# Layer-0 centring in 64x64 blocks, gated GpSimd passes, and half a ladder step moved to GpSimd in a two-layer convolution-shaped kernel

## The chip, the cores and the metric

The kernel runs on one core of a Trainium2 chip. Its engines work side by side, each through its own instructions in order: TensorE (PE, matmuls into PSUM), VectorE (DVE), ScalarE (ACT), GpSimd (POOL), and SyncE (SP), whose queue here issues nearly all DMAs. The metric is the device time of one execution in microseconds; less is better.

## The reference

x has the shape (16, 32, 128, 128). Layer 0 adds to x an attention over its normalised channels. Layer 1 normalises again, cuts each image into windows of 8x8 pixels with 32 channels, normalises over the channels, and runs three small networks on the windows (rows, columns, channels), the sum of which goes through a fourth. Each small network is a layer norm, eight Gaussian bumps of every value, and a matrix:

```python
def _fastkan(x, ln_g, ln_b, ws, wb, bb):
    ln = _layernorm(x, ln_g, ln_b)
    basis = jnp.exp(-((ln[..., None] - GRID) / DENOM) ** 2)
    flat = basis.reshape(*basis.shape[:-2], -1)
    return flat @ ws.T + jax.nn.silu(x) @ wb.T + bb
...
y = _layernorm(wins, pn_g, pn_b)
a = _fastkan(a, k1...)      # y with window columns turned to rows
d = _fastkan(d, k2...)      # y along window rows
e = _fastkan(y.reshape(b, WS * WS, C), k3...)
z = _fastkan((a + d + e).reshape(b, WS * WS, C), k4...)
out = z + wins
...
x = x + _L0_conv_ref(_gn(x), ...)
x = x + _L1_conv_ref(_gn(x), ...)
```

## The kernel before, in words

First, in the ramp, the kernel reads x once for the sums that layer 0's attention needs, and folds the whole attention and the residual into a 256x256 matrix (`pts`) for each half of the batch. The rest is layer 1 with that matrix in front, in 64 units. A unit is 128 partitions (4 images of 32 channels) by 1024 elements (8 image rows of 128 pixels, that is, one row of 16 windows).

A unit goes through these tasks; the names are those of the functions and of the order lists.

- `load` fetches x for two units. `layer0_norm` multiplies by `pts` (L1068), writes the result `xh` (L1078), subtracts the channel mean with a 128x128 matrix (L1083, two matmuls of 512 columns, each recorded as two), copies that to `xc` (L1092), squares it (L1095), and sums the squares (L1036, with Ln and Exp at L1044 and L1045). `keep` sends `xh` to DRAM, and `again` brings it back when the unit ends.
- `rows_norm` makes y from `xc` on VectorE (L1130). GpSimd adds a bias to it in place (L1134) and then writes a second copy with the window columns turned (L1138). Both lie in one tile, `yy`. `move` regroups `yy` by DMA into `d`; `silus` and `move_silu` do the like for the SiLU.
- Chain a (`norm_a`, `scale_a`, `seed_a`, `ladder_a`, `pair_a`) runs the row and column networks on `d`. Chain b runs the channel network of unit n and the fourth network of unit n - 2 together. `norm` centres by matmuls, evicts twice on ScalarE (L1195), squares (L1198), and spreads the scale with matmuls (L1204); `scale` multiplies on VectorE (L1221).
- The bumps are not computed one by one. `seed` makes the first (in chain a also the fifth) on ScalarE, and a ratio R. `ladder` gets each next bump on VectorE from the one before (L1250), 128x2048 elements each: six steps in chain a, seven in chain b. A step is called here by its chain and bump: a1 makes bump 1 of chain a.
- `products` multiplies each bump by its 32x32 weights (L478). `products_a` and `products_b` put a one-element GpSimd memset, a tick, between the matmuls that open a PSUM bank and the others (L1274); `pair_b` has one more (L1410). `pair_b` also adds chain a's result, moved back by DMA, with the 64x64 matmuls `straight` (L1400) and `turned` (L1421).
- `evict_z` copies the three networks' sum to `z`. `result` adds the fourth network to the residual `xh` on VectorE (L1472), and `store` writes it out.

The work of neighbouring units is interleaved. A planner (`Flow`) runs the tasks with estimated times when the program is built and writes each engine's instructions in the order it finds. For the tasks in `ORDER` it does not choose: the table gives each engine's cyclic order as `task.step.units behind`. The tile pools have fixed numbers of buffers; an instruction that needs a buffer, or another engine's result, waits on semaphores.

The ladder step, and the two GpSimd passes over y, are these lines:

```python
STT(t, by, BIG, at, ALU.min, ALU.mult)                                              # L1250
nc.gpsimd.tensor_scalar(y, y, unit, cr["pn_b"], ALU.mult, ALU.add)                  # L1134
nc.gpsimd.tensor_scalar(turned(yy[:, :, 1, :]), straight(y), unit, zero, ...)       # L1138
```

Of the kernel before, what the change touches and what calls it, by code (L numbers as in the profile page):

```python
# [43 lines left out]
LIFT = {"a": 0.0, "b": 80 * math.log(2.0)}  # L44

# [7 lines left out]
LATE = 2  # L53

# [3 lines left out]
        "products_b.3.4 products_b.4.4 products_b.5.4 layer0_norm.0.1 products_b.6.4 products_b.7.4 norm_b.4.3 "  # L58
        "products_b.8.4 products_b.9.4 norm_b.6.3 products_b.10.4 products_b.11.4 layer0_norm.2.1 products_a.0.3 "
        "products_a.2.3 products_a.3.3 layer0_norm.5.1 products_a.4.3 products_a.5.3 norm_a.0.2 products_a.6.3 "  # L60
        "products_a.7.3 norm_b.0.2 products_a.8.3 products_a.9.3 rows_norm.0.1 norm_a.4.2 products_b.0.3 "
        "norm_a.6.2 products_b.2.3 "
    ),
    "ACT": (
        "norm_b.3.3 silus.0.3 seed_a.0.3 seed_a.1.3 seed_a.2.3 norm_b.5.3 layer0_norm.1.1 seed_a.3.3 seed_a.4.3 "
        "evict_z.0.4 seed_b.0.3 layer0_norm.3.1 layer0_norm.4.1 seed_b.1.3 layer0_norm.6.1 seed_b.2.3 norm_a.1.2 "
        "norm_a.2.2 norm_a.3.2 norm_b.1.2 norm_b.2.2 evict_a.0.3 evict_a.1.3 norm_a.5.2 "
    ),
    "DVE": (
        "ladder_a.2.4 ladder_a.3.4 ladder_a.4.4 ladder_a.5.4 ladder_b.0.4 ladder_b.1.4 rows_norm.1.2 ladder_b.2.4 "  # L70
        "scale_a.0.3 scale_a.1.3 ladder_b.3.4 ladder_b.4.4 ladder_b.5.4 ladder_b.6.4 ladder_a.0.3 scale_b.0.3 "
        "scale_b.1.3 result.0.6 ladder_a.1.3 "
    ),
    "SP": (
        "keep.0.1 move.0.2 store.0.6 again.0.5 load.0.0 move_back.0.3 move_silu.0.2 "
    ),
    "POOL": (
        "products_b.1.3 rows_norm.2.1 rows_norm.3.1 products_a.1.2 "
# [173 lines left out]
def conv_preact_kernel(  # L252
# [79 lines left out]
    eps, unit, ones_n = column(), column(), column()  # L332
    nc.vector.memset(eps, EPS)
    nc.vector.memset(unit, 1.0)
    nc.vector.memset(ones_n, 1.0 / S)
    zero, lift = column(), column()
    nc.vector.memset(zero, 0.0)
    nc.vector.memset(lift, LIFT["b"])
# [29 lines left out]
    c0 = const.tile([P, 4, 32], F32, name="c0")  # L368
    TS(c0, quad.unsqueeze(2).to_broadcast([P, 4, 32]), -1.0 / 32, None, ALU.mult)
    TT(c0, c0, ident.rearrange("p (q c) -> p q c", q=4), ALU.add)  # L370
    c0m = c0.rearrange("p q c -> p (q c)")
# [94 lines left out]
    C_R2, C_XB, C_P, C_B0 = range(4)  # L466
# [34 lines left out]
    def layers():  # L501
        with ExitStack() as es:
# [31 lines left out]
            rows3 = lambda t: t.rearrange("p (h w) -> p h w", h=8)  # L534

# [210 lines left out]
            def attention(bp):  # L746
# [258 lines left out]
                STT(qp, gm, cr["k4_bb"], qp, ALU.add, ALU.mult)  # L1005
# [3 lines left out]
                TT(t, t, qp, ALU.add)  # L1009
                for q in range(KK):  # L1010
                    nc.vector.tensor_copy(l0col(bp, q, C_R2), r2[:, q : q + 1])
                    nc.vector.tensor_copy(l0col(bp, q, C_XB), t[:, q : q + 1])
                    for b in range(4):
                        nc.vector.tensor_copy(
                            l0col(bp, q, C_P)[32 * b : 32 * b + 32], p_[32 * (b ^ 1) : 32 * (b ^ 1) + 32, q : q + 1]
                        )
                ps_, = yield step("PE", 0.6, "Y")
                MM(ps_[:, 0, 0:KK], lhsT=c0m, rhs=qp, start=True, stop=True)
                yield step("DVE", 0.3)
                for q in range(KK):  # L1020
                    TS(l0col(bp, q, C_B0), ps_[:, 0, q : q + 1], -1.0, None, ALU.mult)
                give("Y")
# [6 lines left out]
            def rsqrt_rows(src, e, kind):  # L1029

                parts = e.shape[1]
                lr, ve = yield step("PE", 0.24 * parts, kind, "Y")
                for j in range(parts):
                    for c in range(4):
                        u = parts * c + j
                        MM(  # L1036
                            ve[32 * c : 32 * c + 32, 0, 0:P],
                            lhsT=e[:, j, :],
                            rhs=src[:, u * P : (u + 1) * P],
                            start=j == 0,  # L1040
                            stop=j == parts - 1,
                        )
                yield step("ACT", 0.62)
                ACT(lr, ve[:, 0, 0:P], AF.Ln, bias=eps)  # L1044
                ACT(lr, lr, AF.Exp, scale=-0.5)  # L1045
                give("Y")
                return lr
# [13 lines left out]
            def layer0_norm(n):  # L1061
# [19 lines left out]
                xc, yp = yield step("PE", 1.94, "xc", "Y")  # L1081
                for u in range(2):
                    MM(  # L1083
                        yp[:, u, :].rearrange("p (h w n) -> p h n w", h=4, w=8),
                        lhsT=c0m,
                        rhs=xh[:, u * 512 : (u + 1) * 512].rearrange("p (h n w) -> p h n w", h=4, w=8),
                        start=True,
                        stop=True,
                    )
                used(("xh", n), "xh", 2)  # L1090
                yield step("ACT", 1.01, lag=0.0)
                ACT(xc, flat(yp), AF.Identity, bias=l0col(bp, kk, C_B0))  # L1092
                give("Y", LAG)
                sq, = yield step("ACT", 0.96, "n")
                ACT(sq, xc, AF.Square)  # L1095
                lr = yield from rsqrt_rows(sq, e0, "lr0")
                give("n")
                put(("lr0", n), (xc, lr))
# [12 lines left out]
            def rows_norm(n):  # L1111

                yield "get", "parameters"
                xc, lr = yield "get", ("lr0", n)
# [18 lines left out]
                yield step("POOL", 1.29)  # L1133
                nc.gpsimd.tensor_scalar(y, y, unit, cr["pn_b"], ALU.mult, ALU.add)  # L1134
                turned = lambda t: t.rearrange("p w (h n) -> p h w n", h=8)
                straight = lambda t: t.rearrange("p h (w n) -> p h w n", w=8)
                yield step("POOL", 1.29)
                nc.gpsimd.tensor_scalar(turned(yy[:, :, 1, :]), straight(y), unit, zero, ALU.mult, ALU.add)  # L1138
# [86 lines left out]
            def seed(name, n, par):  # L1225
# [3 lines left out]
                for k, i in enumerate(SEEDS[name]):  # L1229
# [8 lines left out]
                    yield step("ACT", 1.9 if LIFT[name] else 1.81, lag=0.0)  # L1238
                    ACT(u, u, AF.Exp, scale=-1.0, **({"bias": lift} if LIFT[name] else {}))  # L1239
                    put(("u", name, n, i), u, LAG)  # L1240

            def ladder(name, n):

                by = yield "get", ("up", name, n)
                for i in range(NG):
                    if i in SEEDS[name]:
                        at = yield "get", ("u", name, n, i)
                        continue
                    t, = yield step("DVE", 2.21, "u", lag=0.0)
                    STT(t, by, BIG, at, ALU.min, ALU.mult)  # L1250
                    used((name, n, i - 1), "u", 2)
                    put(("u", name, n, i), t, LAG)
                    at = t
                give("R", LAG)

# [5 lines left out]
            def products(name, n, wt, also, bank, ws, silus, then, cross):  # L1261
# [14 lines left out]
                for i in range(NG):  # L1276
                    t = yield "get", ("u", name, n, i)
                    yield step("PE", 1.11, lag=0.0)
# [10 lines left out]
                    used((name, n, i), "u", 1 if i + 1 == NG or i + 1 in SEEDS[name] else 2)  # L1289
# [47 lines left out]
            def evict_z(n):  # L1337
                acc = yield "get", ("z_acc", n)
                z, = yield step("ACT", 1.01, "z")
                ACT(z, flat(acc), AF.Identity, bias=cr["k3_bb"])  # L1340
# [14 lines left out]
            def norm_b(n):  # L1355
# [5 lines left out]
                rows = lambda t, h: t[:, 4 * h : 4 * h + 4, 0, :]  # L1361
                cols = lambda t, h: t[:, 512 * h : 512 * h + 512]
                two = (y, rows) if n < N else (z, cols), (z, cols) if n >= BACK else (y, rows)
# [18 lines left out]
            def pair_b(n):  # L1382
# [8 lines left out]
                def straight(acc):  # L1391
# [3 lines left out]
                    for i in range(4):  # L1395
                        v, h = i // 2, i % 2
                        for f in range(2):
# [3 lines left out]
                                    bank(acc, 64 * (f ^ h), 64, 0, h).rearrange("p (l w) -> p l w", l=4)[  # L1401
                                        :, :, 64 * v : 64 * v + 64
                                    ],
                                    lhsT=(near if v else ident)[o, o],
                                    rhs=ar[o, 4 * h : 4 * h + 4, 0, 64 * v : 64 * v + 64],
# [7 lines left out]
                def turned(acc):  # L1413
# [3 lines left out]
                    for h in range(2):  # L1417
                        for f in range(2):
# [3 lines left out]
                                    bank(acc, 64 * (1 ^ f ^ h), 64, 0, h).rearrange("p (h w n) -> p w h n", h=4, w=8),  # L1422
                                    lhsT=(near if h else ident)[o, o],
                                    rhs=ar[o, :, 1, 64 * h : 64 * h + 64].rearrange("p w (h n) -> p w h n", h=4),
# [13 lines left out]
                def silus(o, q):  # L1438
# [5 lines left out]
                    v = mine[o, 4 * h : 4 * h + 4, 0, :] if mine is t else rows3(mine)[o, 4 * h : 4 * h + 4, :]  # L1444
                    return v.rearrange("p h (w n) -> p h w n", w=8) if k else v
# [21 lines left out]
            def result(n):  # L1467
# [3 lines left out]
                yield step("DVE", 1.2)  # L1471
                STT(xh, xh, l0col(bp, kk, C_P), flat(acc), ALU.mult, ALU.add)  # L1472
# [3 lines left out]
            def store(n):  # L1476
                bp, kk, j = units[n]
                xh = yield "get", ("result", n)
                yield step("SP", 2.6, lag=0.0)
                for b in range(4):  # L1480
                    nc.sync.dma_start(
                        out=out_rows[bp * KK + kk, b, :, :, j * RB : (j + 1) * RB],
                        in_=xh[32 * (b ^ 1) : 32 * (b ^ 1) + 32, :],
                    )
                late = fl.moved(1.4, 2.0)
                give("xh", late)

            def again(n):
# [3 lines left out]
                for b in range(4):  # L1492
                    nc.sync.dma_start(out=xh[32 * b : 32 * b + 32, :], in_=xd[32 * (b ^ 1) : 32 * (b ^ 1) + 32, :])
# [5 lines left out]
            with tc.manual_schedule(engines=IN_ORDER):  # L1499
# [23 lines left out]
                        every("keep", keep),  # L1523
                        every("layer0_norm", layer0_norm),
# [88 lines left out]
```

## Time and profile before

| | |
|---|---|
| median of 3 runs | 2687.7 us (2686.57 to 2696.28) |
| profiled execution: its own time | 2688.95 us |
| its span (first to last instruction) | 2687.2 us |
| granted TensorE clock, mean | 0.987 |
| VectorE ladder steps (L1250), 846 in all | 2292 ns each |
| VectorE `scale` (L1221), four a unit | 1214 ns each |
| GpSimd pass L1134 / L1138, median | 2768 / 1200 ns |
| ScalarE Exp on 128x2048 with a bias column / without (L1239) | 1989 / 1904 ns |

A row of the timeline gives the start in us, the duration in us, the engine, the line, the operation, output<-inputs with sizes, and how many instructions of the kind the row merges; in brackets, how long the engine was idle before it and what ended that. A row of the waits gives who waited for whom, then us in total, the number of times and the longest. The pitch of an instruction is the time from its start to the next one's start on the same engine: it can be shorter than its duration, since neighbours overlap by some 0.08 us.

### The profile page before, as it was taken

How to read it: one execution, taken by the hardware profiler on the slowest of the kernel's cores; microseconds unless marked ns; L12 is line 12 of the kernel's file. 1: busy time of each engine (PE TensorE's matmuls, PEld its weight loads, DVE VectorE, ACT ScalarE, POOL GpSimd, SP SyncE). 2: the span in 40 equal slices, each digit the busy share in tenths (PEclk: the TensorE clock that was granted, in tenths of full speed). 3: DMA queues.
4: the chain of work that ended last, by engine and by line, in shares of the span. 5: the costliest groups of instructions: out<-in, count | busy, mean ns of one | idle time of the engine just before them, and what ended most of it. 6: DMA issues, size and time to landing. Idle time of an engine off the chain costs nothing.

```text
span 2687.2 us, 123945 instructions
## 1 busy us (share of the span) xinstructions
PE 2553.4 (95%) x56611; PEld 1300.7 (48%) x56611; DVE 2492.0 (93%) x1637; ACT 2340.5 (87%) x1967; POOL 320.6 (12%) x431
## 2 busy tenths in 40 slices
PE   6998999999999999999999999999999999999975
PEld 6884444444444444444444444444444444444432
DVE  5755799999999999999999999999999999999987
ACT  0016699999999999999999999999999999999973
POOL 4300000111101111101111011111011111011100
PEclk9998999999999999999999999999999999999988
DMA  9752345555555555555555555545555555555421
GB/s 252 189 140 64 104 119 146 144 146 148 146 142 152 151 144 140 144 144 145 147 142 150 143 151 147 146 136 149 141 152 145 142 150 142 150 150 148 135 85 45
DMA packets 289706, 379.71 MB, mean 141 GB/s; under 512 B 42400, under 2 KB 239520, under 8 KB 289184
## 3 DMA queue, kind: packets, MB, share of 16 engines
q1 hardware_dynamic: 275968, 352.48, 47.5%
q10 hardware_dynamic: 9504, 16.85, 2.4%
q8 instruction: 446, 7.31, 1.2%
q0 software_dynamic: 3712, 2.46, 0.4%
q14 instruction: 76, 0.62, 0.1%
HBM read 103.18 MB, written 67.11 MB: 63 GB/s over the span
## 4 chain that ended last, share of the span: by engine, by line
PE 80%; DVE 7%; issue 5%; DMA 1%; ACT 1%; POOL 0%; DVEq 0%; ACTq 0%; POOLq 0%
PE X L478 41%; PE Y L1068 9%; PE Y L1204 5%; PE Y L1083 5%; PE Y L478 4%; PE Y L1036 4%; PE X L498 3%; DVE u L1250 3%; DVE yy L1130 3%; PE Y L1119 2%; PE X L1400 2%; PE X L1421 2%; PE X L733 1%; DMA xh<-xh 1%; DVE yc L1221 0%
## 5 line engine op out<-in xcount | busy, mean ns | idle before, releaser
L1250 DVE SCALAR_TENSOR_TENSOR u<-R,u 128x2048 f32<-128x2048 f32 x846 | 1923.8, 2292 | 54.2 <-PE X L478 5.9
L478 PE MATMUL X<-u,wt_a 32*32 32x512 f32 x16384 | 690.4, 600 | 31.7 <-POOL vec L1274 26.4
L478 PE MATMUL X<-u,wt_b 32*32 32x512 f32 x16896 | 608.1, 601 | 13.0 <-DVE u L1250 12.2
L478 PEld LDWEIGHTS X<-u,wt_a 32*32 32x32 f32 x16384 | 297.5, 103 | 279.1 <-issue 94.9
L1231 ACT ACTIVATE u<-yc,vec 128x2048 f32<-128x2048 f32 x194 | 387.4, 1997 | 24.8 <-DVE yc L1221 17.8
L478 PEld LDWEIGHTS X<-u,wt_b 32*32 32x32 f32 x16896 | 228.0, 103 | 289.1 <-issue 123.1
L1221 DVE TENSOR_TENSOR yc<-yc,Y 128x1024 f32<-128x1024 f32 x260 | 304.9, 1214 | 9.1 <-PE Y L1204 9.0
L1195 ACT ACTIVATE yc<-Y 128x1024 f32<-128x1024 f32 x260 | 251.0, 1018 | 24.1 <-PE Y L478 24.0
L1234 ACT ACTIVATE R<-yc,vec 128x2048 f32<-128x2048 f32 x130 | 258.5, 1988 | 0.0
L1198 ACT ACTIVATE u<-yc 128x2048 f32<-128x2048 f32 x130 | 247.5, 1904 | 2.1
L1239 ACT ACTIVATE u<-u 128x2048 f32<-128x2048 f32 x128 | 243.7, 1904 | 2.0
L1068 PE MATMUL Y<-x,pt 128*128 128x512 f32 x512 | 240.1, 612 | 2.2 <-DVE yy L1130 1.3
L1274 POOL MEMSET vec<- 128x1 f32 x130 | 12.9, 99 | 1524.4 <-PE X L498 1509.7
L1134 POOL TENSOR_SCALAR yy<-yy,vec,col_r 128x1024 f32<-128x1024 f32 x64 | 168.6, 2634 | 157.0 <-DVE yy L1130 132.4
L733 PE MATMUL X<-R 128*64 128x257 f32 (+3 forms) x2048 | 151.5, 308 | 24.0 <-DVE R L707 22.4
L1068 PEld LDWEIGHTS Y<-x,pt 128*128 128x128 f32 x512 | 93.2, 192 | 147.0 <-issue 143.0
L733 PEld LDWEIGHTS X<-R 128*64 128x64 f32 x2048 | 140.7, 140 | 38.0 <-DVE R L707 25.1
L1317 ACT ACTIVATE ad<-X,col 128x1024 f32<-128x1024 f32 x128 | 135.7, 1120 | 0.3 <-PE X L478 0.2
L1239 ACT ACTIVATE u<-u,vec 128x2048 f32<-128x2048 f32 x66 | 131.3, 1989 | 0.0
L478 PE MATMUL Y<-yy,c 32*32 32x512 f32 x1056 | 129.2, 598 | 1.2 <-DVE att L894 1.2
L1083 PE MATMUL Y<-xh,c 128*128 128x512 f32 x256 | 129.3, 628 | 1.0 <-DVE yc L1221 0.7
L1152 ACT ACTIVATE S<-yy 128x2048 f32<-128x2048 f32 x64 | 122.5, 1913 | 0.7
(224 smaller groups left out, 2825.7 us busy)
## 6 DMA issues: line engine op xcount, KB each, us to landing
xh<-xh SPq DMA_DIRECT2D x512, 128.0 KB
d<-yy SPq DMA_DIRECT2D x512, 128.0 KB
sd<-S SPq DMA_DIRECT2D x512, 128.0 KB
ad_r<-ad SPq DMA_DIRECT2D x512, 128.0 KB
x<-in_x SPq DMA_DIRECT2D x256, 128.0 KB
out<-xh SPq DMA_DIRECT2D x256, 128.0 KB
u<-in_x ACTq DMA_DIRECT2D x28, 256.0 KB
u<-in_x SPq DMA_DIRECT2D x28, 256.0 KB
```

Of the source, the lines that this page charges most:

```text
L478: MM(dst(to, g_), lhsT=wt[32 * g_ : 32 * g_ + 32, :], rhs=rhs(g_, to ^ cross[g_]), start=start, stop=stop,)
L733: MM(g[64 * q : 64 * q + 64, k, lo:hi], lhsT=t[:, b, at : at + 64], rhs=t[:, b, lo:hi], start=first, stop=last,)
L1068: MM(xp[:, u, :], lhsT=pts[bp][:, k, kk * P : (kk + 1) * P], rhs=xr[:, k, u * 512 : (u + 1) * 512], start=k == 0, stop=k == KK - 1,)
L1083: MM(yp[:, u, :].rearrange("p (h w n) -> p h n w", h=4, w=8), lhsT=c0m, rhs=xh[:, u * 512 : (u + 1) * 512].rearrange("p (h n w) -> p h n w ...
L1134: nc.gpsimd.tensor_scalar(y, y, unit, cr["pn_b"], ALU.mult, ALU.add)
L1195: ACT(v[:, i * RB : (i + 1) * RB], flat(yt[i]), AF.Identity)
L1198: ACT(sq, v, AF.Square)
L1221: TT(v[:, o], v[:, o], flat(rb[i]), ALU.mult)
L1231: ACT(u, v, AF.Square, bias=bqs[k])
L1234: ACT(up, v, AF.Exp, bias=bp_, scale=2.0)
L1239: ACT(u, u, AF.Exp, scale=-1.0, **({"bias": lift} if LIFT[name] else {}))
L1250: STT(t, by, BIG, at, ALU.min, ALU.mult)
```

## The change

1. Layer-0 centring. The 128x128 matrix `c0m` gives way to 64x64 blocks (`c0w`, one for each half of the batch and channel group), so that four tiles of TensorE work on 512 columns each. The block carries a scale of 1/(1 + sd), and `xh` is scaled so that `result` needs no multiplication. The two halves of the columns come out with partition halves exchanged in one of them; `straight`, `turned`, `norm_b`'s operands, `silus`' operands, `evict_z`, `again`, `result` and `store` follow that layout. `turned` issues 8 matmuls of 256 columns for 4 of 512, `result` 2 instructions of 512 for one of 1024, `store` 8 DMAs for 4 of twice the size.
2. ScalarE squares from PSUM, before a new task `centre` copies to `xc`; the two were the other way round.
3. GpSimd's passes over y. The turned copy comes first and includes the bias; from the third unit on it waits for ladder step b3 of two units earlier (in chain order it is the step just before `scale_a`). The in-place pass follows later.
4. Ladder step a2 is split. VectorE does the second 1024 of the 2048 columns; a new GpSimd task `assist` does the first 1024 in two instructions, a min and a product, after step a1.
5. Bias columns that hold a constant become immediates (Ln, and chain b's seed Exp).
6. `ORDER` is new. GpSimd's cycle is: turned copy, min, in-place pass, product, two ticks.

```diff
+HALVES = {"a": (2,), "b": ()}
+EARLY = 3
+GATE = ("b", 3)
     "DVE": (
-        "ladder_a.2.4 ladder_a.3.4 ... scale_b.1.3 result.0.6 ladder_a.1.3 "
+        "ladder_b.0.6 ladder_b.1.6 rows_norm.1.4 ladder_b.2.6 scale_a.0.5 scale_a.1.5 ladder_b.3.6 ladder_b.4.6 "
+        "ladder_b.5.6 ladder_b.6.6 ladder_a.0.5 scale_b.0.5 scale_b.1.5 result.0.8 ladder_a.1.5 ladder_a.2.5 "
+        "ladder_a.3.5 ladder_a.4.5 ladder_a.5.5 "
     "SP": (
-        "keep.0.1 move.0.2 store.0.6 again.0.5 load.0.0 move_back.0.3 move_silu.0.2 "
+        "store.0.7 keep.0.2 again.0.6 move_back.0.4 move_silu.0.3 load.0.0 move.0.2 "
     "POOL": (
-        "products_b.1.3 rows_norm.2.1 rows_norm.3.1 products_a.1.2 "
+        "rows_norm.2.3 assist.0.4 rows_norm.3.3 assist.1.4 products_a.1.4 products_b.1.4 "
...
-                ACT(lr, ve[:, 0, 0:P], AF.Ln, bias=eps)
+                ACT(lr, ve[:, 0, 0:P], AF.Ln, bias=EPS)
...
                 for u in range(2):
-                    MM(
-                        yp[:, u, :].rearrange("p (h w n) -> p h n w", h=4, w=8),
-                        lhsT=c0m,
-                        rhs=xh[:, u * 512 : (u + 1) * 512].rearrange("p (h n w) -> p h n w", h=4, w=8),
+                    for f in range(2):
+                        o = slice(64 * f, 64 * f + 64)
+                        MM(
+                            yp[64 * (f ^ u) : 64 * (f ^ u) + 64, u, :].rearrange("p (h w m) -> p h m w", h=8, w=8),
+                            lhsT=c0w[o, bp, kk, :],
+                            rhs=xh[o].rearrange("p (h u m w) -> p u h m w", h=8, u=2, m=8)[:, u],
...
-                ACT(xc, flat(yp), AF.Identity, bias=l0col(bp, kk, C_B0))
-                ACT(sq, xc, AF.Square)
+                ACT(windows(sq), chunks(yp), AF.Square)
+            def centre(n):
+                xc, = yield step("ACT", 1.01, "xc")
+                nc.scalar.copy(windows(xc), chunks(yp))
...
-                nc.gpsimd.tensor_scalar(y, y, unit, cr["pn_b"], ALU.mult, ALU.add)
-                nc.gpsimd.tensor_scalar(turned(yy[:, :, 1, :]), straight(y), unit, zero, ALU.mult, ALU.add)
+                add = nc.gpsimd.tensor_scalar(turned(yy[:, :, 1, :]), straight(y), unit, cr["pn_b"], ALU.mult, ALU.add)
+                if n >= EARLY:
+                    after([add], [before])
+                nc.gpsimd.tensor_scalar(y, y, unit, cr["pn_b"], ALU.mult, ALU.add)
...
+                    if i in HALVES[name]:
+                        t = yield "get", ("open", name, n, i)
+                        yield step("DVE", 1.15, lag=0.0)
+                        STT(t[:, RB:], by[:, RB:], BIG, at[:, RB:], ALU.min, ALU.mult)
+            def assist(n):
+                rc, = yield step("POOL", 1.2, "att", lag=0.0)
+                after([nc.gpsimd.tensor_scalar(rc, by[:, 0:RB], BIG, None, ALU.min)], [before])
+                t, = yield step("POOL", 2.35, "u")
+                nc.gpsimd.tensor_tensor(t[:, 0:RB], rc, at[:, 0:RB], ALU.mult)
...
-                STT(xh, xh, l0col(bp, kk, C_P), flat(acc), ALU.mult, ALU.add)
+                for h, c in enumerate((C_B, C_BX)):
+                    o = slice(512 * h, 512 * h + 512)
+                    STT(xh[:, o], xh[:, o], l0col(bp, kk, c), acc[:, h, :], ALU.add, ALU.add)
```

## The prediction

> **What bounds the kernel now.** I read the page first, then a table by stretches, the waits of the steady part, then the two engines the change trades between, instruction by instruction.
>
> ```profile
> span 2687.2 us, 123945 instructions
> PE 2553.4 (95%) x56611; PEld 1300.7 (48%) x56611; DVE 2492.0 (93%) x1637; ACT 2340.5 (87%) x1967; POOL 320.6 (12%) x431
> ```
>
> The shares include ramp and tail; a steady stretch (columns PE, PEld, DVE, ACT, POOL busy, clock, DMA share, GB/s) says more:
>
> ```profile
> 1500.00:1900.00 400.00, 390.61 (x9048) 187.86 (x9032) 392.35 (x208) 390.29 (x325) 46.65 (x55) 1.00 0.53 147
> ```
>
> Three engines are 97 to 98% busy at full clock. So who waits for whom (us in total, times, longest; 700 to 2300 us, 43.5 units):
>
> ```profile
> PEld X L478 <- DVE u L1250: 75.9, 132, 0.8
> ACT lr L1044 <- PE Y L1036: 27.5, 45, 1.2
> PE X L478 <- POOL vec L1274: 18.4, 43, 0.5
> PE Y L1204 <- DVE yy L1130: 17.4, 43, 0.8
> DVE yc L1221 <- PE Y L1204: 1.2, 4, 0.4
> ```
>
> The others wait for VectorE; VectorE waits for nobody. Its order over one unit:
>
> ```profile
> 1505.43 1.21 DVE L1130 TENSOR_TENSOR yy<-xc,Y 128x1024 f32<-128x1024 f32 x1
> 1506.56 2.29 DVE L1250 SCALAR_TENSOR_TENSOR u<-R,u 128x2048 f32<-128x2048 f32 x1
> 1508.77 2.35 DVE L1221 TENSOR_TENSOR yc<-yc,Y 128x1024 f32<-128x1024 f32 x2
> 1511.03 11.72 DVE L1250 SCALAR_TENSOR_TENSOR u<-R,u 128x2048 f32<-128x2048 f32 x5
> 1522.66 2.35 DVE L1221 TENSOR_TENSOR yc<-yc,Y 128x1024 f32<-128x1024 f32 x2
> 1524.92 1.27 DVE L1472 SCALAR_TENSOR_TENSOR xh<-xh,l0c,X 128x1024 f32<-128x1024 f32 x1
> 1526.12 16.20 DVE L1250 SCALAR_TENSOR_TENSOR u<-R,u 128x2048 f32<-128x2048 f32 x7
> 1542.24 1.21 DVE L1130 TENSOR_TENSOR yy<-xc,Y 128x1024 f32<-128x1024 f32 x1
> ```
>
> Back to back: 1542.24 - 1505.43 = 36.81 us a unit, all of it VectorE. TensorE's need is 36.8 less its two waits (18.4 + 17.4)/43 = 0.8: 36.0. ScalarE's is 36.8 - 27.5/43 = 36.2. About 60 units run at this pace (from 365 us to 2540).
>
> GpSimd has room, but look at how it runs beside VectorE:
>
> ```profile
> 1507.15 2.77 POOL L1134 TENSOR_SCALAR yy<-yy,vec,col_r 128x1024 f32<-128x1024 f32 x1 [0.39 <-DMA xh<-xh]
> 1510.02 1.20 POOL L1138 TENSOR_SCALAR yy<-yy,vec 128x1024 f32<-128x1024 f32 x1
> ```
>
> Same size, 2.77 against 1.20. The first begins inside the ladder step of 1506.56 and makes no progress until that step is over (1508.85): 1.07 us later it is done. The second runs at full speed beside L1221, which reads one operand from PSUM. And the other way round, once, in the ramp:
>
> ```profile
> 233.79 2.59 DVE L1250 SCALAR_TENSOR_TENSOR u<-R,u 128x2048 f32<-128x2048 f32 x1 [0.84 <-ACT u L1239]
> 233.05 1.20 POOL L1134 TENSOR_SCALAR yy<-yy,vec,col_r 128x1024 f32<-128x1024 f32 x1 [47.33 <-DVE yy L1130]
> ```
>
> Here GpSimd came first, kept its 1.20 us, and the ladder step took 2.59 instead of 2.29: held up 0.30, to 234.09, that is 0.15 before GpSimd's recorded end. In the steady part the 0.04 by which the step of 1511.03 is stretched (2.33) is the same, with L1138 ending at 1511.22. So whichever of the two starts first excludes the other. The Trainium skill says so too (SBUF — State Buffer, SBUF: two separate sides).
>
> **The change part by part**, per unit.
>
> *VectorE.* Half a ladder step leaves. Two halves of size 1024 differ by 2.29 - 1.21 (L1250 against L1221), so 1.07 less. `result` becomes two of 512: L1472 goes from a pitch of 1.20 to 2 x 0.67 (0.53 of streaming and its 0.13 fixed), 0.13 more. The half step is followed by step 3, which waits for it and for GpSimd; the ladder's dependent pitch with two waits is 2.39 where this pair's was 2.32: 0.07 more. The 0.04 of L1138 goes, since GpSimd's first pass is now gated to the end of step b3 and fits beside the two `scale_a` (1.20 in 2.26). Sum -0.83; summing the new order pitch by pitch I get 35.91, so -0.89, which I use.
>
> *The wait that comes.* GpSimd's order becomes: turned copy (gated), tick, min (gated to the end of ladder step a1), the y pass, the product, two ticks. The y pass now stands between min and product. Time from the start of a1: VectorE's a1 takes a pitch of 2.20, two `scale_b` 2.26, two `result` 1.33, so the half step could start at 5.80 and step 3 at 7.12. GpSimd: a1 ends at 2.29; with 0.10 between its instructions (1509.92 to 1510.02) min is 2.39 to 3.59, the y pass 3.69 to 4.89, both beside VectorE work with a PSUM operand. The product starts at 4.99, before the half step, and reads two SBUF tensors, so the half step waits for it.
>
> How long is that product? The trace has no tensor_tensor on GpSimd. The nearest row is L1138: 1.20 for 1024 elements, but with one streamed input. By the row the product ends at 6.19, the half step waits 6.19 - 0.15 - 5.80 = 0.24, and the unit changes by -0.65: 39 us faster in all. The Trainium skill (GPSIMD Engine Reference, Performance versus the Vector engine) speaks against this: two inputs share one read port, about 2.6 cycles an element at 1.2 GHz, 4497 ns for 2048. For 1024 my estimate from that is 2.25 (half) to 2.54 (2.22 and L1138's fixed 0.32). I take 2.4, because the second input is a second stream that L1138 lacks. Then the product ends at 7.39, the half step waits 7.24 - 5.80 = 1.44, and the unit changes by -0.89 + 1.44 = +0.55. With 2.25 it is +0.40, with 2.54 +0.69. Break-even is a product of 1.85.
>
> *TensorE.* Centring: L1083 takes 1.98 for its four records (1524.53 to 1526.51 on the chain); four 64x64 tiles over 512 columns are what L1421 issues now, 1.08 (1522.42 to 1523.5). -0.90. `turned` becomes eight half-width matmuls like L1400's (1.09): nothing. New operand strides in runs of 8: no row; 0 to 0.2 each, taken 0. TensorE's need falls to 35.1; it is not the bound, so worth 0 here.
>
> *ScalarE.* A bias column costs 0.085 (L1239: 1989 with, 1904 without). Gone from three Ln, one Exp and the xc copy; the Square reads PSUM (1018 like L1195, was 1059): about -0.47, to 35.7. Also hidden behind VectorE, worth 0; uncovered it would be a bound 0.2 below VectorE's 35.9, so no gain of more than 1.1 a unit is possible in any case. Writing in runs of 8: taken 0.
>
> *Queues.* SP's `store` goes from 4 DMAs (3.01) to 8 half-size ones (6.0). A unit with a load fills SP for 32.6 now, 35.6 then, still under the period. `move` waits for the y pass, which ends at 4.89 instead of long before: on the clock above 1525.4 instead of 1523.0, behind the load in SP. It issues for 5.65, to 1531.0; `norm_a` took the data at 1532.6. That leaves 1.6 for landing; if late, up to 1 us of TensorE's 2 us and ScalarE's 1.6 of slack at the longer period covers it. GpSimd's tick for products_a now stands behind the product (7.49, or 1527.95, against 1527.87): 0.1, covered likewise. `centre` holds a PSUM buffer 1 us longer, but Ln already ended that stretch at 1532. The set-up loses a matmul and gains four small VectorE passes: under 2 us, taken 0.
>
> **Sum.** 60 x 0.55 = +33 us on the profiled execution's 2688.95 (span 2687.2 and 1.75 around it); the median of the runs shown is 1.25 lower, so 2687.7 + 33 = 2721. About 0.5% (13 us) is what a measurement of this kernel can tell from no change.
>
> **The rivals.**
> *The product does not hold up the half step* (it is as cheap as L1138, or two-input operations interleave). For: only one instance of GpSimd coming first by a margin is in the trace, none with this operation. Against: that instance, and all the 2.77s. By the cheap product 39 us faster, 2649; with a product of 2.4 beside the half step, step 3 waits until 7.49 instead of 7.12, the unit changes by -0.89 + 0.37 = -0.52, 31 us faster: 2657. Chance 0.20.
> *Both gains and waits cancel*: a product of 1.7 to 2.0, -0.15 to +0.15 a unit, 2679 to 2697. Chance 0.09.
> *The half step wins the race.* If GpSimd's start, min or y pass takes 0.81 longer in all, the half step runs first and the product stands still until about 6.95, ends at 9.35, and step 3 starts at 9.4 instead of 7.12: -0.89 + 2.3 = +1.4, 2772. For: spans on GpSimd are rough. Against: L1138's 1.20 with a spread of 0.01. Chance 0.08.
> *It is as reckoned*: 0.63, with 2.25 to 2.54 for the product and 0.1 for what I took as 0: 2708 to 2735.
>
> **How the numbers follow.** Faster 0.20, same 0.09, slower 0.63 + 0.08 = 0.71. Range 2655 to 2740: it leaves out the race (0.08) and about half of the faster case.
>
> **What would show it.** Right: the half step's instruction (1024 elements) lasts about 2.6 instead of 1.2, its end 0.1 after the product's; the product about 2.4; period 37.3; TensorE and ScalarE with more waits for VectorE. L1134's successor at 1.2, not 2.77. Wrong: a half step of 1.2; or VectorE with waits for TensorE or ScalarE, which would put the bound elsewhere; or a step 3 that starts long after the half step.

## The result and the profile after

The changed kernel takes 2837.1 us (median of 4 runs, 2833.7 to 2841.0) against 2692.0 for the one before (4 runs): a ratio of 1.0544, with a 95% interval of 1.0516 to 1.0573. It is slower, as forecast, but by 145 us where 33 were forecast, and outside the range (its upper end was 2740). The page of the changed kernel, and its steady stretch (PE, PEld, DVE, ACT, POOL busy, clock, DMA share, GB/s):

```profile
span 2839.1 us, 126157 instructions
PE 2549.1 (90%) x57375; PEld 1322.0 (47%) x57375; DVE 2454.8 (86%) x1696; ACT 2307.0 (81%) x1967; POOL 610.4 (22%) x559
```

```profile
1500.00:1900.00 400.00, 369.19 (x8736) 181.90 (x8736) 365.81 (x206) 363.97 (x310) 87.54 (x72) 0.99 0.54 137
```

No engine is full any more: three that were 97 to 98% busy are at 91 to 92%. GpSimd's two new lines in the page's groups (count, busy us, mean ns, idle before):

```profile
L1291 POOL TENSOR_SCALAR att<-R 128x1024 f32<-128x1024 f32 x64 | 178.1, 2783 | 163.0 <-DVE u L1271 136.7
L1293 POOL TENSOR_TENSOR u<-att,u 128x1024 f32<-128x1024 f32 x64 | 207.6, 3243 | 0.2
```

The min (L1291) takes 2.77 us where 1.20 was reckoned, in all but one of 64 cases within 2.76 to 2.79; the next pass starts 2.87 after it in the rows below, so the length is not only that of a recorded span. The product (L1293) is 2.34 to 2.38 when nothing is in its way, as reckoned. The half step is L1268 here, the other ladder steps are L1271, `scale` is L1235, `result` L1528, the turned copy L1148 and the y pass, the in-place one, L1152. One unit's VectorE and GpSimd around them, from the timeline (start, duration):

```profile
1558.07 2.35 DVE L1235 TENSOR_TENSOR yc<-yc,Y 128x1024 f32<-128x1024 f32 x2
1560.33 1.40 DVE L1528 SCALAR_TENSOR_TENSOR xh<-xh,l0c,X 128x512 f32<-128x512 f32 x2
1561.64 1.72 DVE L1268 SCALAR_TENSOR_TENSOR u<-R,u 128x1024 f32<-128x1024 f32 x1
1565.62 6.89 DVE L1271 SCALAR_TENSOR_TENSOR u<-R,u 128x2048 f32<-128x2048 f32 x3 [2.25 <-POOL vec L1317]
```

```profile
1558.23 2.77 POOL L1291 TENSOR_SCALAR att<-R 128x1024 f32<-128x1024 f32 x1 [2.41 <-DVE u L1271]
1561.10 1.20 POOL L1152 TENSOR_SCALAR yy<-yy,vec,col_r 128x1024 f32<-128x1024 f32 x1
1562.26 3.32 POOL L1293 TENSOR_TENSOR u<-att,u 128x1024 f32<-128x1024 f32 x1
```

The min runs into the time of `result`, so the y pass (L1152) is still on when the half step (L1268, 1561.64) comes: that waits 0.5 for it (1.72 instead of 1.22). By then the product has begun too, and stands still until the half step is through (3.32 instead of 2.38). Step a3 starts at 1565.62, 3.97 after the half step, where 1.32 is its own. In about half of the units `scale_b` comes some 0.6 later, the half step then starts with the product, and it is 3.47. In three of 64 the product wins, which makes the half step 3.2 to 3.5 long.

The waits between 800 and 2400 us (41 units), engines and SP's queue, point to a second loss:

```profile
ACT yc L1209 <- PE Y L481: 118.7, 41, 4.8
PE Y L481 <- DMA d<-yy: 19.7, 14, 2.3
DVE u L1271 <- POOL vec L1317: 85.5, 38, 2.3
DVE yc L1235 <- PE Y L1218: 14.7, 36, 0.8
SPq L1192 <- POOL yy L1152: 96.9, 27, 6.5
```

SP waits 96.9/41 = 2.4 us a unit for the y pass before it can issue `move` (L1192); TensorE then waits for d, and ScalarE stands 118.7/41 = 2.9 us a unit for `norm_a`'s result. An engine with slack may stand without loss; what costs is that VectorE, too, waits for the spread scale of the two `scale` steps, 14.7/41 = 0.4 us a unit. Its wait for L1317, GpSimd's tick that follows the product, 85.5/41 = 2.1, is the product's.

The 152 us between the two profiled spans lie as follows, by the starts of `rows_norm` on VectorE (units counted from 0):

| stretch | before | after | more |
|---|---|---|---|
| to unit 6 | 436.3 | 448.2 | 12 |
| unit 6 to 63 | 2100.9 (36.86 each) | 2219.9 (38.95 each) | 119 |
| from unit 63 to the end | 149.9 | 171.0 | 21 |

### The profile page after: what moved, and what is told of

The parts are those of the page before. It is cut to its first block, busy times and chain, and to the rows that moved or that the text cites. A ratio compares the mean times of both kernels' runs of the same rounds, so it can differ in the third digit from the quotient of the medians.

```text
span 2839.1 us, 126157 instructions
## 1 busy us (share of the span) xinstructions
PE 2549.1 (90%) x57375; PEld 1322.0 (47%) x57375; DVE 2454.8 (86%) x1696; ACT 2307.0 (81%) x1967; POOL 610.4 (22%) x559
## 4 chain that ended last, share of the span: by engine, by line
PE 30%; DVE 28%; POOL 13%; issue 9%; SPq 6%; ACT 5%; DMA 4%; DVEq 0%; ACTq 0%; POOLq 0%
DVE u L1271 24%; PE X L481 15%; POOL u L1293 5%; POOL att L1291 5%; PE Y L481 3%; DVE yc L1235 3%; SPq L1192 2%; POOL yy L1152 2%; PE Y L1036 2%; PE Y L1218 2%; PE Y L1068 2%; DMA out<-xh 2%; PE X L501 2%; DMA d<-yy 2%; PE X L738 1%
## 5 line engine op out<-in xcount | busy, mean ns | idle before, releaser
L1271 DVE SCALAR_TENSOR_TENSOR u<-R,u 128x2048 f32<-128x2048 f32 x782 | 1774.5, 2289 | 194.8 <-POOL vec L1317 132.9
L481 PE MATMUL X<-u,wt_a 32*32 32x512 f32 x16384 | 681.7, 622 | 122.0 <-POOL vec L1317 105.7
L481 PEld LDWEIGHTS X<-u,wt_a 32*32 32x32 f32 x16384 | 323.8, 105 | 360.6 <-issue 145.1
L1253 ACT ACTIVATE u<-u 128x2048 f32<-128x2048 f32 x194 | 368.9, 1902 | 2.0
L1235 DVE TENSOR_TENSOR yc<-yc,Y 128x1024 f32<-128x1024 f32 x260 | 305.3, 1215 | 41.1 <-PE Y L1218 40.4
L1317 POOL MEMSET vec<- 128x1 f32 x130 | 12.6, 97 | 1093.5 <-PE X L501 1093.5
L1291 POOL TENSOR_SCALAR att<-R 128x1024 f32<-128x1024 f32 x64 | 178.1, 2783 | 163.0 <-DVE u L1271 136.7
L1293 POOL TENSOR_TENSOR u<-att,u 128x1024 f32<-128x1024 f32 x64 | 207.6, 3243 | 0.2
L1457 POOL MEMSET vec<- 128x1 f32 x64 | 6.3, 99 | 678.9 <-PE X L1445 678.9
L481 PE MATMUL Y<-d,c 32*32 32x512 f32 x2048 | 83.8, 634 | 53.9 <-issue 24.7
L1148 POOL TENSOR_SCALAR yy<-yy,vec,col_r 128x1024 f32<-128x1024 f32 x64 | 79.8, 1246 | 205.2 <-DVE yy L1140 122.9
```

What stands on the lines that cost most here:

```text
L481: MM(dst(to, g_), lhsT=wt[32 * g_ : 32 * g_ + 32, :], rhs=rhs(g_, to ^ cross[g_]), start=start, stop=stop,)
L1235: TT(v[:, o], v[:, o], flat(rb[i]), ALU.mult)
L1253: ACT(u, u, AF.Exp, scale=-1.0, bias=LIFT[name])
L1271: laid = STT(t, by, BIG, at, ALU.min, ALU.mult)
L1291: after([nc.gpsimd.tensor_scalar(rc, by[:, 0:RB], BIG, None, ALU.min)], [before])
L1293: nc.gpsimd.tensor_tensor(t[:, 0:RB], rc, at[:, 0:RB], ALU.mult)
```

## The experiments

In the table, "a unit" is the mean distance of `rows_norm` on VectorE in the steady part; "a2 to a3" is the mean distance from the start of step a2 (half or whole) to the next step, 20 to 46 units; the own time of a half step there is 1.32, of a whole one 2.32. Each ratio is to the kernel before as it ran beside that kernel (medians 2688.8 to 2692.6). In the code, "..." stands for lines left out.

| kernel | us | ratio to before (95%) | a unit | a2 to a3 |
|---|---|---|---|---|
| before | | 1 | 36.86 | 2.32 |
| changed | 2837.1 | 1.0544 (1.0516 to 1.0573) | 38.96 | 3.67 |
| e1 whole step | 2704.9 | 1.0052 (1.0036 to 1.0069) | 37.25 | 2.32 |
| e2 y pass first | 2767.1 | 1.0279 (1.0263 to 1.0294) | 37.89 | 3.01 |
| e3 cheap pass for min | 2777.2 | 1.0318 (1.0286 to 1.0350) | 37.80 | 2.19 |
| e4 min with columns | 2875.8 | 1.0702 (1.0684 to 1.0720) | 39.57 | 4.38 |
| e5 no min, y pass first | 2682.3 | 0.9971 (0.9958 to 0.9985) | 36.60 | 1.33 |
| e6 whole step, late y pass | 2727.2 | 1.0136 (1.0110 to 1.0162) | 37.45 | 2.32 |
| e7 e5, move_back first | 2690.6 | 0.9997 (0.9988 to 1.0005) | 36.84 | 1.33 |
| e8 e7 without gate | 2685.0 | 0.9987 (0.9978 to 0.9996) | 36.74 | 1.33 |
| e10 e8, move before load | 2639.9 | 0.9811 (0.9797 to 0.9825) | 35.99 | 1.33 |
| e12 e10, again late | 2933.1 | 1.0909 (1.0888 to 1.0929) | 41.08 | 1.33 |
| e13 changed, queue of e10 | 2840.5 | 1.0553 (1.0533 to 1.0572) | 38.83 | 3.72 |
| e14 whole step, queue of e10, no gate | 2688.5 | 0.9985 (0.9976 to 0.9994) | 36.97 | 2.32 |

**The split undone (e1).**

```diff
-HALVES = {"a": (2,), "b": ()}
+HALVES = {"a": (), "b": ()}
-        "rows_norm.2.3 assist.0.4 rows_norm.3.3 assist.1.4 products_a.1.4 products_b.1.4 "
+        "rows_norm.2.3 rows_norm.3.3 products_a.1.4 products_b.1.4 "
...
-                        every("assist", assist),
```

> The change without the split: step a2 is whole on VectorE again, the min and the product on GpSimd are gone, and the y pass follows the gated turned copy at once. Theory A (the min takes 2.77 instead of 1.2, so min, y pass and product hold up the half step and step a3 by 2.2 to 2.6 us a unit): the wait is gone; VectorE has its 36.8 of before, 0.13 more for the two result halves, and up to 0.28 where the y pass reaches into step b4: about 37.1 a unit, 2695 to 2715 us. Rival B (the new column layout, the exchanged order of y passes or the new order of the engines costs the time, the split little): stays above 2780 us, with waits of TensorE and ScalarE as in the changed kernel.

2704.9: 132 of the 145 us are gone, so the loss comes with the split and the order on GpSimd that it brings. The rest, 0.39 a unit against before, is VectorE's own: step b4, which the y pass reaches into, has 0.30 more (2.73 from its start to the next, before 2.43), and the two halves of `result` 0.13.

**The y pass ahead of the min (e2).**

```diff
-        "rows_norm.2.3 assist.0.4 rows_norm.3.3 assist.1.4 products_a.1.4 products_b.1.4 "
+        "rows_norm.2.3 rows_norm.3.3 assist.0.4 assist.1.4 products_a.1.4 products_b.1.4 "
```

> The changed kernel, but GpSimd does the in-place y pass right behind the turned copy, before the min. Theory A: min from 2.39 to 5.16 after the start of step a1, product 5.26 to 7.64, ahead of the half step, which waits until 7.49 instead of 5.80: 1.7 a unit, and 0.28 where the y pass reaches into step b4; about 37.9 a unit against the measured 38.96, 2765 to 2785 us. Rival C (the late y pass, which makes the move to d, norm_a and scale_a late, is the main cost): nearly all comes back, 2690 to 2715 us.

2767.1 and 37.89 a unit, as theory A reckoned (37.9). One unit of it:

```profile
1561.05 2.90 DVE L1268 SCALAR_TENSOR_TENSOR u<-R,u 128x1024 f32<-128x1024 f32 x1
1557.64 2.76 POOL L1291 TENSOR_SCALAR att<-R 128x1024 f32<-128x1024 f32 x1 [2.57 <-DVE u L1271]
1560.49 2.37 POOL L1293 TENSOR_TENSOR u<-att,u 128x1024 f32<-128x1024 f32 x1
```

The product comes first, and the half step lasts 2.90. Step a3 comes 3.01 after the half step's start, 1.69 more than its own 1.32: the time from 5.80 to the product's end. With the min at 2.77 the steady period adds up: 35.91, 0.28 at step b4 and 1.69 make 37.88. VectorE's waits for TensorE, 22.2 us in the changed kernel between 800 and 2400 us, are 0.5 us here.

**A cheap pass in the place of the min (e3), and the min in the cheap pass's form (e4).** A column here is an operand with one value per partition.

```diff
-after([nc.gpsimd.tensor_scalar(rc, by[:, 0:RB], BIG, None, ALU.min)], [before])
+after([nc.gpsimd.tensor_scalar(rc, by[:, 0:RB], unit, zero, ALU.mult, ALU.add)], [before])   # e3
+after([nc.gpsimd.tensor_scalar(rc, by[:, 0:RB], unit, big, ALU.mult, ALU.min)], [before])    # e4
...                                         # e4: a column `big` that holds BIG
```

> The changed kernel with the min replaced by a multiplication by 1 and addition of 0 in the form of the y pass (the bound on R is left out in that half). Theory A (the min itself is slow): the pass takes 1.20, the product starts at 4.99, the half step waits 1.44 as the prediction reckoned: 37.35 a unit plus up to 0.4 of the late y pass, 2720 to 2750 us. Rival D (whatever GpSimd does at that place takes 2.77, because of what VectorE does beside it): the pass takes 2.77 again, 2825 to 2845 us.

> The changed kernel with its min kept, but written like the cheap pass: multiplication by 1 and then min, both operands from columns, so that only the second operation differs from the cheap pass. If the min operation itself is slow on GpSimd: 2.7 or more for 1024 elements, and 2825 to 2850 us as the changed kernel. If the one-operation form with an immediate was slow: 1.20, and 2765 to 2790 us as the cheap pass, with the bound kept.

GpSimd's groups, first of e3, then of e4, where the min is at L1293 (800 to 2400 us):

```profile
L1291 POOL TENSOR_SCALAR att<-R,vec 128x1024 f32<-128x1024 f32 x43 | 51.4, 1196 | 80.6 <-DVE u L1271 80.6
L1293 POOL TENSOR_TENSOR u<-att,u 128x1024 f32<-128x1024 f32 x43 | 101.8, 2368 | 0.0
```

```profile
L1293 POOL TENSOR_SCALAR att<-R,vec 128x1024 f32<-128x1024 f32 x40 | 151.1, 3777 | 68.4 <-DVE u L1273 68.4
```

At the same place, with the same tiles and the same kind of operands, multiply-add takes 1196 ns and multiply-min 3777; the change's min alone takes 2767. So it is the min, not the place and not the form. e4's time, 2875.8, is 26 us above what was expected of a slow min, since this form of it is slower still.

e3 (2777.2) shows the rest too: with the pass at 1.20 and the product at 2.37, the half step is held up 0.87 (2.19 against 1.32). That is less than the 1.44 of the prediction for two reasons. GpSimd's three instructions start 1.17 apart and not 1.30, so the product begins 4.72 after step a1's start, 0.27 sooner than reckoned; and `scale_b` now comes 0.3 late, which GpSimd does not wait for. The unit lands at 37.80, 0.4 above the prediction's 37.4, with further waits ahead of step b1, of `rows_norm` and of both scales. The time is 27 us above the upper end of what theory A expected: in the profiled execution, the fastest of the four at 2767.8, ramp and tail together are 26 us longer than before, and theory A has no place for them.

**The y pass late, by itself (e6).**

```diff
 # on the whole-step kernel e1
+                    late = yield "get", ("late", n - 1)         # step a1
...
-                nc.gpsimd.tensor_scalar(y, y, unit, cr["pn_b"], ALU.mult, ALU.add)
+                pass2 = nc.gpsimd.tensor_scalar(y, y, unit, cr["pn_b"], ALU.mult, ALU.add)
+                    after([pass2], [late])
```

> As the whole-step kernel, but the in-place y pass waits for the end of ladder step a1, as late as in the changed kernel; GpSimd has nothing else there and runs beside scale_b, so no lock on VectorE. What is late alone is the y pass, with the move to d behind it. Theory C1 (the prediction's: covered by slack): VectorE's own 36.94, since step b4 no longer loses 0.33; 2688 to 2706 us, not slower than the whole-step kernel's 2704.9. Theory C2 (not covered: the move, norm_a and the two scale steps run late, as the 1.0 us of other waits a unit in the cheap-pass kernel suggest): 37.5 to 37.9 a unit, 2720 to 2750 us.

2727.2: slower than e1 by 22 us although step b4 gets its 0.33 back, so the late y pass costs 0.5 a unit in the steady part (37.45 against the 36.94 that VectorE needs), and the tail is 14 us longer. That is C2, at its low end. The waits show the way it takes, and SP's queue where it begins (800 to 2400 us):

```profile
ACT yc L1213 <- PE Y L481: 41.8, 28, 4.0
PE Y L481 <- DMA d<-yy: 10.3, 5, 3.0
SPq L1196 <- POOL yy L1154: 41.3, 19, 3.3
```

**Neither min nor late y pass (e5).**

```diff
-                after([nc.gpsimd.tensor_scalar(rc, by[:, 0:RB], BIG, None, ALU.min)], [before])
-                nc.gpsimd.tensor_tensor(t[:, 0:RB], rc, at[:, 0:RB], ALU.mult)
+                after([nc.gpsimd.tensor_tensor(t[:, 0:RB], by[:, 0:RB], at[:, 0:RB], ALU.mult)], [before])
...
-        "rows_norm.2.3 assist.0.4 rows_norm.3.3 assist.1.4 products_a.1.4 products_b.1.4 "
+        "rows_norm.2.3 rows_norm.3.3 assist.0.4 products_a.1.4 products_b.1.4 "
```

> The changed kernel without the min (the product reads R directly, so the bound on R is left out in that half) and with the y pass right behind the turned copy. Theory A: the product runs from 2.39 to 4.77, beside work that has a PSUM operand, the half step is free at 5.80; VectorE 35.91 plus 0.28 for the y pass, 36.2 a unit against 36.86 before: 2645 to 2665 us, faster than before. Rival E (ScalarE or TensorE with the new layout becomes the bound, or the ramp and tail of the changed order, 33 us longer, stay): 2685 to 2720 us.

The lock is gone (1.33 from a2 to a3), and yet it takes 2682.3, 17 us over the upper end of what theory A gave: 36.60 a unit, though 22 of 57 units take theory A's 36.2. Something else holds the others.

**What else: SP's queue (e7, e8, e10, e12).** All four build on e5; the last three also leave the gate out. SP's waits of e5 pointed at the `store`, whose landing `again` (L1550) waits for:

```profile
SPq L1550 <- DMA out<-xh: 210.9, 87, 4.5
```

```diff
-        "store.0.7 keep.0.2 again.0.6 move_back.0.4 move_silu.0.3 load.0.0 move.0.2 "
+        "store.0.7 keep.0.2 move_back.0.4 again.0.6 move_silu.0.3 load.0.0 move.0.2 "   # e7, e8
+        "store.0.7 keep.0.2 move_back.0.4 again.0.6 move_silu.0.3 move.0.2 load.0.0 "   # e10
+        "store.0.7 keep.0.2 move_back.0.4 move_silu.0.3 move.0.2 again.0.6 load.0.0 "   # e12
-EARLY = 3
+EARLY = 10**9                                                                           # e8, e10, e12: no gate
```

> The kernel without min and with the y pass first, and on SP's queue move_back ahead of again. Theory F (again waits 4.9 us a unit for the landing of the store's eight DMAs, move_back stands behind it, so straight and then scale_b are late: 2.40 instead of 2.20 there): scale_b comes on time, 36.58 a unit falls to 36.2 to 36.4, 2658 to 2674 us. Rival G (TensorE or ScalarE is simply full at 36.6): no change, 2677 to 2689 us.

Theory F falls: `scale_b` is as late as before (2.42 after the start of a1, where 2.20 is on time), and the median is not better but 8 us worse. (The execution that was profiled took 2704.0, 13 above the median, so the table's 36.84 is somewhat high.) The largest wait in a queue was not the one that counted.

> The same without the gate on the turned copy, which then starts inside step b3, stands still until its end, and finishes 1.07 after it, as L1134 did before. If the gate costs its hand-over (step b4 waits 0.2 for the y pass): about 0.15 a unit less than with the gate, 8 to 12 us less. If the gate was needed (the pass would start ahead of step b3 or sooner and hold VectorE up): 0.3 to 1 a unit more, 15 us or more above it.

Step b4 comes back to 2.41 from 2.60, as reckoned; part of that is lost again to the other waits: 2685.0, 6 us less where 8 to 12 were expected. Here, where the y pass follows at once, the gate is not needed. Units now lie between 35.93, which is VectorE's own time, and 39. SP's queue of e8 in a unit with a load, and e10's, where `move` (L1192) was put ahead of the `load` (L1058):

```profile
1557.41 4.62 SPq L1058 DMA_DIRECT2D x<-in_x  x8
1562.14 5.66 SPq L1192 DMA_DIRECT2D d<-yy  x8
```

```profile
1527.69 6.04 SPq L1192 DMA_DIRECT2D d<-yy  x8
1533.84 4.84 SPq L1058 DMA_DIRECT2D x<-in_x  x8
```

> The no-gate kernel with move ahead of load on SP's queue. Theory H (in units with a load, move stands behind its eight DMAs, d lands late, and norm_a, ScalarE and the scale steps follow; units of 38 to 39 us come from this): those units go, 36.74 a unit falls to 36.3 to 36.5, 2660 to 2675 us. Rival E (the ring of TensorE's stretch from rb_a to evict_z and ScalarE's from evict_z to the next rb_a, about 36.5 us as the trace adds up, is the bound): little, 2675 to 2687 us, and units of 36.78 stay the commonest.

2639.9, 20 us below what theory H gave, and rival E is refuted: the ring of TensorE and ScalarE that I had added up to 36.5 closes in 35.99. 51 of 57 units take 35.93 to 36.0. The swap issues `move` sooner and `load` later; the two were not tried apart. VectorE's timeline of one of them, and GpSimd's:

```profile
1512.81 1.21 DVE L1140 TENSOR_TENSOR yy<-xc,Y 128x1024 f32<-128x1024 f32 x1
1513.94 2.28 DVE L1271 SCALAR_TENSOR_TENSOR u<-R,u 128x2048 f32<-128x2048 f32 x1
1516.14 2.34 DVE L1235 TENSOR_TENSOR yc<-yc,Y 128x1024 f32<-128x1024 f32 x2
1518.40 11.71 DVE L1271 SCALAR_TENSOR_TENSOR u<-R,u 128x2048 f32<-128x2048 f32 x5
1530.03 2.35 DVE L1235 TENSOR_TENSOR yc<-yc,Y 128x1024 f32<-128x1024 f32 x2
1532.29 1.40 DVE L1525 SCALAR_TENSOR_TENSOR xh<-xh,l0c,X 128x512 f32<-128x512 f32 x2
1533.61 1.22 DVE L1268 SCALAR_TENSOR_TENSOR u<-R,u 128x1024 f32<-128x1024 f32 x1
```

```profile
1514.73 2.56 POOL L1148 TENSOR_SCALAR yy<-yy,vec,col_r 128x1024 f32<-128x1024 f32 x1 [0.34 <-issue]
1517.39 1.20 POOL L1152 TENSOR_SCALAR yy<-yy,vec,col_r 128x1024 f32<-128x1024 f32 x1
1530.20 2.38 POOL L1291 TENSOR_TENSOR u<-R,u 128x1024 f32<-128x1024 f32 x1 [2.33 <-DVE u L1271]
```

The product (1530.20 to 1532.58) lies wholly beside `scale_b` and `result`, the half step is 1.22 long, and VectorE is back to back. This kernel is faster than the changed one and, by 1.9%, than the one before. It leaves out the bound on R in the half that GpSimd makes.

> The same, with again and load both behind move_back, move_silu and move, so that nothing on SP's queue that waits for a landing stands before a transfer that TensorE waits for. Theory H: at least as good as the kernel before it, 2655 to 2672 us. Rival E: the same 2675 to 2687 us.

Both theories missed: 2933.1, the slowest of all. With `again`, which brings the residual back, behind `move_silu` and `move`, the residual comes late, and `result` on VectorE waits for it, 133.4/39 = 3.4 us a unit (800 to 2400 us):

```profile
DVE xh L1525 <- DMA xh<-xh: 133.4, 41, 4.6
PE X L501 <- DVE xh L1525: 114.9, 39, 4.2
```

**Is the queue what the change lacked, or the split what makes e10 fast (e13, e14)?** e13 is the changed kernel with e10's SP order, e14 the whole-step kernel e1 with that order and `EARLY = 10**9`.

> The changed kernel with SP's queue of the fastest kernel so far (move_back ahead of again, move ahead of load), nothing else. Theory J (in the changed kernel move waits for the late y pass, which ends after the load is issued, so the queue's order is not what delays it): half step and step a3 as before, 38.7 to 39.0 a unit, 2820 to 2845 us. Rival K (the queue's order costs the changed kernel too): the 0.65 a unit of waits other than the half step's goes, 38.3 a unit, 2795 to 2812 us.

> The whole-step kernel (no split, the bound on R everywhere) without the gate and with that queue. If the split without min is what makes the fastest kernel faster: VectorE's own 36.94 a unit, 2685 to 2697 us. If the queue and the gate are: 36.0 to 36.3, 2640 to 2660 us.

e13: 2840.5, theory J. In the changed kernel `move` waits for the late y pass anyway, so its place in the queue makes no difference. e14: 2688.5 and 36.97 a unit, which is VectorE's own 36.94. Its gain over e1, 0.28 a unit, is step b4's (2.73 to 2.43) and so the missing gate's; the queue had little to give there, since VectorE's waits in e1 are 1.4 us in 1600. From there the split without the min takes the unit to 35.99. Queue and split are worth little without each other: with the split, e8 had 36.74; with the queue, e14 36.97.

## Why the prediction was wrong, point by point

- *The bound and the lock.* Right. VectorE bounds the kernel before; in the changed one its work and its waits for GpSimd's product make the period. A GpSimd operation and a two-input ladder step exclude each other: 1.72 for 1.22 and 3.32 for 2.38 in the rows above. "Slower" came out by another way than the one forecast, though: the product was to hold up the half step, and it starts ahead of it in three of 64 units only.
- *VectorE's own work, 35.91 a unit.* Right: e10's units take 35.93 at the least. (The parts listed ahead of it add up to -0.91, not -0.83: the 0.04 of L1138 has the wrong sign there; the 35.91 does not rest on it. The low end of "as reckoned" would be 2706, not 2708.)
- *TensorE's centring, 0.90 less.* Right: L1085 takes 44.7/41 = 1.09 a unit where L1083 took 1.98. It is hidden, as said.
- *The product, 2.4.* Right: 2.34 to 2.38 undisturbed, and 2.38 in e10. The rule of the Trainium skill on two inputs (GPSIMD Engine Reference, Performance versus the Vector engine) gave the size, and the row of L1138 would have been half of it.
- *"min is 2.39 to 3.59".* This is the step that failed. The min was given L1138's 1.20 since it too streams one input; it takes 2.77. I had bounded the product from two sides and the min not at all. The trace had no row for a min on GpSimd, and the nearest row has other operations. With 2.77 the chain min, y pass, product is due 1.57 later; measured, the product starts 6.40 after step a1's start, where 4.99 was reckoned.
- *Which of the two goes first.* The rival "the half step wins the race" named the point, 0.81 of extra time ahead of the product; the min used 1.57. It was given 0.08, against "L1138's 1.20 with a spread of 0.01", which says nothing of another operation. Its price was too low as well: +1.4 a unit, while the units that show it alone (16 of 57) are 38.53, +1.67 over before. It had left out that the half step also waits for the y pass.
- *"if late ... slack at the longer period covers it".* The second step that failed. The late y pass costs 0.5 a unit by itself (e6), and in the changed kernel the unit is 0.4 above 38.53. The slack of TensorE and ScalarE was counted over a whole unit; but `norm_a`, the evictions, the spreading of the scale and `scale` are a chain with a due time, and ScalarE cannot fill its wait for `norm_a` with other work, since its order is fixed. That is read from the waits; no run loosened ScalarE's order.
- *Queues.* The eight `store` DMAs fitted into SP's time, as said. That `load` now stands before `move` was noted; its effect, with the y pass early, was not: e10 against e8 puts it at 0.75 a unit. In the changed kernel it was hidden by the late y pass (e13).
- *How the two failed steps share the 145 us.* With a cheap pass for the min 60 us go (e3), with the y pass ahead, which also lets the product start 1.2 sooner, 70 (e2), with the y pass ahead and no min at all 155 (e5). So the min's length is not the whole of it: e3, whose pass takes the 1.20 that was reckoned, is at 2777 still above the range.
- *60 x the unit's difference.* The 57 units from 6 to 63 have 119 of the 152 us, 2.1 each; ramp and tail add 33, taken as 0. The tail is longer wherever the y pass is late or the min is there (161 to 174 us in e2, e3, e4, e6, e13), 155 to 158 with the split alone (e5, e7, e8, e10, e12), and 147 to 150 without any of them (e1, e14, before). Why was not tried.

Two things are left open: no run has e10's queue with the gate, so the gate's own share there is not known; and why multiply-min is 1.01 slower than min alone.

## What to carry to other kernels

An operation moved to an engine that has not run it before has no price until a row of that operation gives one: bound every instruction of the moved step from both sides, not only the one that looks dear. Work that shares a lock has to fit whole into the stretch where the other engine does not want it, in the order in which it will be issued; here one unrelated pass between its two instructions delayed both the pass and the product. When a gain fails to show after the suspected stall is gone, read the DMA queue's order for a transfer that waits behind one that nobody needs yet, and move only that: here, putting the residual's transfer behind as well cost 11% (e12).

## What the runs showed of the hardware that was not expected

GpSimd's tensor_scalar on 128x1024 f32 depends strongly on the operation: 1.20 us for multiply-add with two columns (e3), 2.77 for min with an immediate (the changed kernel, e2), 3.78 for multiply-min with two columns (e4). In 25 of the changed kernel's 64 units the half step and the product are recorded as starting within 12 ns of each other. VectorE goes first in 24 of them: the half step keeps its 1.22, and the product takes 3.43 instead of 2.37. In the other one the product, 12 ns ahead, does. An Ln on 128x128 from PSUM takes 275 ns with an immediate bias (changed kernel) against 367 with a column (before), close to the 85 ns that the prediction took from another line.
